# Pair sums on VectorE, regrouped basis products, and a new order at the start and the ends of norms in a four-layer graph network kernel

## The chip, the cores and the metric

The kernel runs on one core of one Trainium2 chip. A core has TensorE (matmuls; PE in the profile, its weight loads PEld), VectorE (DVE), ScalarE (ACT), GpSimd (POOL) and SyncE (SP), and 16 DMA engines that carry what the queues of SP, ACT and POOL issue. The metric is the device time of one execution in microseconds; the median of several runs is compared.

## The reference, cut to what matters

512 nodes with 512 features, 16896 edges, four residual layers, each behind a layer norm and a relu (`h = relu(norm(x))`):

```python
# layer 0: attention over edges, softmax over axis 1 (the HEADS), then a feed-forward net
scores = einsum('nhd,mhd->nhm', q, k) / sqrt(64)          # 8 heads
scores = where(adj[:, None, :] == 0, -1e9, scores)
attn = softmax(scores, axis=1)
h1 = layer_norm(h + einsum('nhm,mhd->nhd', attn, v) @ Wo + bo, g1, be1)
x += layer_norm(h1 + relu(h1 @ W1 + b1) @ W2 + b2, g2, be2)
# layer 1: twice  segment_sum over edges, two linear maps, batch norm, relu, residual
# layer 2: segment_sum with 1/sqrt(degree) on both sides, one linear map
# layer 3: two gated relational layers, for r in 0, 1:
w = einsum('rb,bio->rio', att, basis)                      # 30 bases of 512 x 512
gate = sigmoid(x_j @ gate_w[r]);  msg_r = gate * x_j @ w[r]
out = segment_sum(msg by edge type) + x @ root + bias
```

Because the softmax goes over the 8 heads, its denominator for a pair of nodes is the sum of 8 numbers that lie in 8 different slices of a tile.

## The kernel before, in words

The edges become a 512 x 512 matrix of counts for each edge type. **Start**: the edge indexes (`idx`, `idx2`, the last 4 of 132 chunks) and `x` are loaded, indexes are transposed into `key`, `look_for_strays` sets a flag, and every engine branches on it (L440; the branch is not taken here). The first norm (`norm_relu`) and its four transposes (`flip`) make `hT`. **Counting**: 204 count matmuls (L535) of one-hot rows that VectorE (`hd`, L522, and 3 of 7 `hs`, L528) and ScalarE (4 of 7 `hs`, L526) make. The loop over `order` is a schedule written out by hand: at count numbers in `products` a step of the q, k, v projections is issued, at those in `groups` one step of bases, at those in `begun` the first steps of attention.

**Attention** runs over 8 blocks (2 halves of the queries by 4 tiles of keys). Pass j of its loop issues `weigh(j)` (L630 reciprocal, L631 product, VectorE), `scores(j+2)` (L600, L606 and ScalarE copies), `values(j-1)` (L641), one or two basis steps, `sums(j+1)` (L626: each head's 128 x 256 slice times the identity, added up in one PSUM bank), and `shift(j+2)` (L614 to L621: maximum, subtraction, exponent).

**Bases.** Half of the 30 bases (layer 1 of the gated layers) and 22 (layer 2) are combined on TensorE: a `basis_step` (L244) is 8 matmul instructions; two steps (layer 1) or three (layer 2) close the one PSUM bank `bas`, which ScalarE copies out (L249) before the next step can start, and DMA writes to `summed`. There are 40 steps, strewn over the program. The other bases are added on VectorE: `accumulate` (L268), 1.2 us each, drawn with `advance(more, n)`. Both draw from one ring of four tiles, filled by SP in the order of `USES`.

**Later stages.** Feed-forward; then `gather` (L874: rounded matmuls into four banks `acc`, inside a branch of `exactly`), copies to `aT`, two linear maps, norms with `settle` for layer 1; a gather again for layer 2; then `Layer` twice for layer 3: `look` (gate sums with `gate_rows`, L751 to L754), `begin` (root products, L1014), `messages` (gated halves L1025 and L1026, products L320, copies L1039 and L1041), `end` (L1048).

**What sets the order.** A scheduler orders each engine's instructions by program place and readiness. Those passed through `on` (or `tc.keep_in_program_order`) keep their order among themselves on their engine; the others may be moved. A conditional block is placed as a whole.

Of the kernel before, what the change touches and what calls it, by code (L numbers as in the profile page):

```python
# [17 lines left out]
P = 128  # L18
# [15 lines left out]
USES = "P" * 26 + "VPVVVPPPVPVVPPVVVVPPPPPPPVVVVVVVVVVVV"  # L34
# [40 lines left out]
def gnn_kernel(ctx: ExitStack, tc: tile.TileContext, out: bass.AP, a: dict):  # L75
# [41 lines left out]
    for i, name in enumerate(("dst", "src", "edge_type_2")):  # L117
        nc.sync.dma_start(idx[:, i, :], a[name][0:P * P].rearrange("(c p) -> c p", p=P))
        nc.sync.dma_start(idx2[:, i, :], a[name][P * P:E].rearrange("(c p) -> c p", p=P))
    x = const.tile([P, T, D], F32, name="x")  # L120
    for t in range(T):
        nc.scalar.dma_start(x[:, t, :], a["x"][t * P:(t + 1) * P, :])
# [33 lines left out]
    nc.gpsimd.memset(apart, 1.0)  # L156
# [184 lines left out]

    def stats(v):

        st = stat("st", 6)
        nc.vector.bn_stats(st, v)  # L345
        mv = stat("mv", 2)
        nc.vector.bn_aggr(mv, st)  # L347
        sd = stat("sd")
        nc.scalar.activation(sd, mv[:, 1:2], AF.Sqrt, bias=eps)  # L349
        rstd = stat("rstd")  # L350
        nc.vector.reciprocal(rstd, sd)
        return mv[:, 0:1], rstd
# [16 lines left out]
    far_off = const.tile([P, P], BF16, name="far_off")  # L369
    nc.vector.tensor_scalar(far_off, ident, FAR, None, op0=ALU.mult)  # L370
    deg = const.tile([P, T], F32, name="deg")

    iot = ep.tile([P, N], F16, name="iot")
    nc.vector.tensor_copy(iot, it)
# [4 lines left out]
    for ix, c0 in ((idx, 0), (idx2, P)):  # L379
        n = ix.shape[0]  # L380
        kn = rp.tile([n, 3, P], F32, name=f"kn{c0}")
        nc.vector.tensor_copy(kn, ix)
        for i in range(3):
            nc.tensor.transpose(pk[:, i, c0:c0 + n], kn[:, i, :], ident[:n, :n])
    nc.vector.tensor_copy(key[:, 0:2, :], pk[:, 0:2, :])
    nc.vector.tensor_scalar(key[:, 2, :], pk[:, 2, :], 0.0, LESS, op0=ALU.is_equal, op1=ALU.max)
    nc.vector.tensor_scalar(key[:, 3, :], key[:, 1, :], -1.0, 0.5, op0=ALU.mult, op1=ALU.add)
# [5 lines left out]
    def look_for_strays():  # L393
        over = rp.tile([P, NCH], F32, name="over")
        nc.vector.tensor_tensor(stray, key[:, 0, :], lim[:, 0, :], ALU.is_lt)
        nc.vector.tensor_tensor(over, key[:, 0, :], lim[:, 1, :], ALU.is_ge)
        nc.vector.tensor_add(stray, stray, over)
        some = rp.tile([P, 1], F32, name="some")
        nc.vector.tensor_reduce(some, stray, AX.X, ALU.max)
        p = ps()  # L400
        nc.tensor.matmul(p[0:1, 0:1], lhsT=some, rhs=ones, start=True, stop=True)
        nc.vector.tensor_copy(flag, p[0:1, 0:1])
# [35 lines left out]
    look_for_strays()  # L438
    strays = nc.values_load(flag[0:1, 0:1])
# [5 lines left out]
    made["h"], made["hT"] = big("A"), big("B")  # L445
    for t in range(T):
        norm_relu(made["h"][:, t, :], x[:, t, :])
# [140 lines left out]
    class Block:  # L588
# [33 lines left out]

        def sums(self):
            self.total = bank("ps")[:, :NH]
            for j in range(H):
                on(nc.tensor.matmul(self.total, lhsT=ident, rhs=self.sc[:, j, :], start=(j == 0), stop=(j == H - 1)))  # L626
# [38 lines left out]
    groups = (40, 55, 70, 84, 98, 109, 118, 126, 137, 148, 162, 180, 190)  # L665
    shifts = [None, None]

    def shift_step(i):
        if shifts[i] is None:
# [5 lines left out]
             148: lambda: shift_step(1), 162: lambda: shift_step(1), 184: lambda: blocks[0].sums()}  # L675
# [26 lines left out]
    for j, block in enumerate(blocks):  # L702
        block.weigh()
        if j + 2 < len(blocks):
            blocks[j + 2].scores()
        if j:
            blocks[j - 1].values()
        if j + 1 < len(blocks):
            basis_step(2 if j in (0, 2) else 1)
            blocks[j + 1].sums()  # L710
        if j + 2 < len(blocks):
            for _ in blocks[j + 2].shift():
                pass
# [30 lines left out]
    def gate_rows(l):  # L744

        out = []
        for r in range(2):
            p = ps()
            for k in range(T):
                at = (GW1, GW2)[l] + 2 * k + r  # L750
                nc.tensor.matmul(p[:, ts(k)], lhsT=cols[:, at:at + 1].to_broadcast([P, P]), rhs=ident,  # L751
                                 start=True, stop=True)
            row = rpool.tile([P, 512], F32, tag="row", name="row")
            nc.scalar.copy(row, p)  # L754
            out.append(row)
        return out
# [111 lines left out]
    def gather(ks):  # L868

        def emit(f, c):  # L870
            for k in ks:
                for m in range(T):
                    for i in range(2):
                        nc.tensor.matmul(acc[m], lhsT=f(xn[i][:, k, ts(m)]), rhs=Clx[c][:, k, :],  # L874
                                         start=(k == 0 and i == 0), stop=(k == T - 1 and i == 1))
# [21 lines left out]
    for l in range(2):  # L897
# [50 lines left out]
        if l == 0:  # L948
            settle(l, h2T, 2, xn)
            basis_step(2)  # L950
            settle(l, h2T, 3, xn)
        else:
# [4 lines left out]
            basis_step(1)  # L957

# [23 lines left out]
    first_w = gate_rows(0)  # L982
# [13 lines left out]
    class Layer:  # L996
# [20 lines left out]
        def messages(self, tg, tu, beside):  # L1017
# [11 lines left out]
            for r in range(2):  # L1029
                o = big(tu[r])  # L1030
                for m in range(T):
# [10 lines left out]
                    advance(beside)  # L1042
# [18 lines left out]
    for t in range(1, T):  # L1061
        first.begin(t)
        advance(more, 2)
# [9 lines left out]
    second = Layer(big("A"), big("B"), gate_rows(1))  # L1073
# [11 lines left out]
    for t in (2, 3):  # L1085
        second.begin(t)
        advance(more2, 2)
# [50 lines left out]
```

## Time and profile before

| what | us |
|---|---|
| runs: median (lowest, highest) | 531.04 (528.6, 534.85) |
| the profiled execution, its span | 529.36, 527.6 |
| PE busy | 490.3 (93%) |
| PEld, DVE, ACT, POOL busy | 258.6, 395.3, 195.6, 37.8 |
| start, to the first projection matmul (L459) | 0 to 22 |
| counting | 19 to 111 |
| attention, to the last L626 | 112 to 178 |
| output projection, feed-forward | 178 to 263 |
| layer 1 of the network, layer 2 | 265 to 362, 363 to 397 |
| gated layers | 397 to 524 |

The span is the time between the first and last instruction of the trace; the rest of the profiled time lies around it. The profile's chain of work that ended last goes through TensorE for 69% of the span, VectorE 13%, ScalarE 6%. The DMA engines are busy for 92 to 96% between 40 and 80 us, 62 to 67% in most of attention. The granted TensorE clock is 1.00 in every stretch but 360 to 400 us (0.91) and 400 to 440 us (0.96). A busy PE includes matmuls that wait inside the pipeline, so the distance from one matmul's start to the next is the better measure of its rate.

### The profile page before, as it was taken

Reading aid. Unit: us, or ns where it says so; the run is one execution under the profiler, and the core shown is the slowest. Engines: PE = TensorE matmul, PEld = TensorE weight load, DVE = VectorE, ACT = ScalarE, POOL = GpSimd, SP = SyncE. Lnnn points to the kernel's source line nnn. Section 1 sums busy time; section 2 is a strip of 40 time slices with the busy share of each in tenths; the row PEclk is TensorE's granted clock in tenths of the full one; section 3 lists DMA queues with packets and bytes.
Section 4 is the critical chain, followed back from the end, with each engine's and each line's share of the span. In section 5 each row is a group of like instructions: output and inputs, shape, how many; then the busy total and the mean of one; then the engine's idle time right before and its main releaser. Section 6 shows DMA issues by size and latency. Waiting matters only on the chain.

```text
span 527.6 us, 5796 instructions
## 1 busy us (share of the span) xinstructions
PE 490.3 (93%) x2046; PEld 258.6 (49%) x2046; DVE 395.3 (75%) x738; ACT 195.6 (37%) x318; POOL 37.8 (7%) x81
## 2 busy tenths in 40 slices
PE   1799998799999999999999898999699899999996
PEld 1333343256556546874445344544543385446642
DVE  3855577869897678999786686796579997998611
ACT  3587758753443213224231225124516311123000
POOL 6000000000000011210040000000010100000000
PEclk9999999999999999999999999999799989999999
DMA  7999989798655579768482875766807986420011
GB/s 244 260 219 246 239 237 227 197 249 204 145 128 116 123 161 284 269 174 213 125 255 81 253 235 160 229 174 173 202 2 226 325 203 232 151 89 1 2 40 40
DMA packets 43033, 94.06 MB, mean 178 GB/s; under 512 B 2124, under 2 KB 2520, under 8 KB 43000
## 3 DMA queue, kind: packets, MB, share of 16 engines
q1 hardware_dynamic: 34408, 67.32, 47.9%
q0 software_dynamic: 5712, 21.07, 14.1%
q10 hardware_dynamic: 2880, 5.24, 2.9%
q8 instruction: 20, 0.33, 0.3%
q14 instruction: 13, 0.11, 0.1%
HBM read 88.38 MB, written 5.24 MB: 177 GB/s over the span
## 4 chain that ended last, share of the span: by engine, by line
PE 69%; DVE 13%; issue 7%; ACT 6%; POOL 0%; DMA 0%; ACTq 0%; POOLq 0%; DVEq 0%
PE pr L320 12%; PE acc L1048 10%; PE pg L320 7%; PE ps L626 6%; PE bas L244 5%; PE ps L459 4%; DVE wrel L268 4%; PE acc L874 3%; PE ao L641 3%; PE psc L606 3%; PE acc L1014 3%; PE ao L535 2%; ACT hs L526 2%; DVE st L345 2%; PE acc L320 1%
## 5 line engine op out<-in xcount | busy, mean ns | idle before, releaser
L268 DVE SCALAR_TENSOR_TENSOR wrel<-basis,scal,wrel 128x1024 f32<-128x1024 f32 x60 | 74.1, 1284 | 0.0
L526 ACT ACTIVATE hs<-iot,key 128x512 f16<-128x512 f16 x75 | 48.3, 711 | 7.1 <-PE ao L535 5.4
L522 DVE TENSOR_SCALAR hd<-iot,key 128x32 f16<-128x32 f16 (+1 forms) x132 | 33.3, 295 | 22.2 <-PE ao L535 22.1
L244 PE MATMUL bas<-basis,wide 120*32 120x512 f32 (+1 forms) x320 | 43.7, 600 | 0.9 <-ACT sums L249 0.9
L268 DVE SCALAR_TENSOR_TENSOR w<-basis,scal,w 128x1024 f32<-128x1024 f32 x32 | 39.5, 1279 | 0.9 <-issue 0.9
L535 PE MATMUL ao<-hs,hd 128*32 128x512 f16 x204 | 24.6, 392 | 5.9 <-DVE Bc L544 2.2
L626 PE MATMUL ps<-sc,ident 128*128 128x256 f32 x128 | 29.8, 386 | 0.0
L349 ACT ACTIVATE sd<-mv,eps 128x1 f32<-128x1 f32 x32 | 9.2, 293 | 55.1 <-DVE mv L347 54.1
L626 PEld LDWEIGHTS ps<-sc,ident 128*128 128x128 f32 x128 | 23.7, 190 | 9.5 <-issue 5.8
L621 ACT ACTIVATE sc<-sc 128x2048 f32<-128x2048 f32 (+1 forms) x10 | 15.7, 1567 | 29.5 <-DVE sc L620 29.5
L459 PE MATMUL ps<-bigB,w 128*128 128x512 f32 x56 | 25.9, 605 | 0.0
L320 PE MATMUL pr<-bigE,w 128*128 128x512 f32 x48 | 21.4, 596 | 1.7 <-ACT bigE L913 1.7
L535 PEld LDWEIGHTS <-hd 128*32 128x32 f16 x204 | 7.7, 95 | 26.4 <-issue 15.9
L1094 DVE TENSOR_TENSOR u<-acc,x 128x512 f32<-128x512 f32 x4 | 2.8, 691 | 23.5 <-PE acc L1048 23.5
L320 PE MATMUL pr<-bigD,w 128*128 128x256 f32 x88 | 20.2, 380 | 0.0
L528 DVE TENSOR_SCALAR hs<-iot,key 128x512 f16<-128x512 f16 x57 | 19.6, 353 | 0.4 <-DVEq L440 0.4
L630 DVE RECIPROCAL rec<-ps 128x256 f32<-128x256 f32 x8 | 14.0, 1755 | 7.5 <-PE ps L626 7.5
L620 DVE TENSOR_TENSOR sc<-sc,half 128x2048 f32<-128x2048 f32 (+1 forms) x10 | 18.6, 1863 | 0.2
L608 ACT COPY sc<-psc 128x1024 f32<-128x1024 f32 x16 | 15.9, 1009 | 7.2 <-PE psc L606 5.6
L631 DVE TENSOR_TENSOR sc<-sc,rec 128x2048 f32<-128x2048 f32 x8 | 18.3, 2292 | 0.3
L606 PE MATMUL psc<-bigC,bigD 64*128 64x256 f32 x128 | 18.2, 402 | 0.0
L320 PEld LDWEIGHTS pr<-bigD,w 128*128 128x128 f32 x88 | 16.6, 190 | 3.0 <-ACT bigE L819 0.8
(302 smaller groups left out, 944.9 us busy)
## 6 DMA issues: line engine op xcount, KB each, us to landing
basis<-in_basis SPq DMA_DIRECT2D x32, 960.0 KB
basis<-in_basis SPq DMA_DIRECT2D x23, 1024.0 KB
basis<-in_basis SPq DMA_DIRECT2D x16, 448.0 KB
summed<-sums ACTq DMA_DIRECT2D x16, 256.0 KB
w<-in_W POOLq DMA_DIRECT2D x4, 1024.0 KB, 6.2
row<-in_rows POOLq DMA_DIRECT2D x12, 256.0 KB, 7.6
wrel<-summed POOLq DMA_DIRECT2D x4, 512.0 KB, 8.0
w<-in_conv_W1T POOLq DMA_DIRECT2D x2, 1024.0 KB, 5.8
```

Of the source, the lines that this page charges most:

```text
L244: tc.keep_in_program_order(nc.tensor.matmul(sums[0][32 * j:32 * j + 32, :], lhsT=lhsT, rhs=t[:k, j, :], start=(g == 0), stop=(g == STEPS + ...
L268: on(nc.vector.scalar_tensor_tensor(to[r][:, i:i + 2, :], t[:, i:i + 2, :], scal[:, at:at + 1], to[r][:, i:i + 2, :], op0=ALU.mult, op1=AL ...
L320: nc.tensor.matmul(p, lhsT=lhsT, rhs=rhs, start=(i == 0), stop=(i == len(pairs) - 1))
L459: on(nc.tensor.matmul(p, lhsT=w[:, k, ts(m)], rhs=made["hT"][:, k, :], start=(k == 0), stop=(k == T - 1)))
L522: keep(nc.vector.tensor_scalar(hd[:, :w], iot[:, GW * groups_of[c][0]:GW * groups_of[c][0] + w], key[:, 0, c:c + 1], key[:, 2, c:c + 1], o ...
L526: keep(nc.scalar.activation(hs, iot, AF.Sign, bias=key[:, 3, c:c + 1]))
L528: keep(nc.vector.tensor_scalar(hs, iot, key[:, 1, c:c + 1], None, op0=ALU.is_equal))
L535: keep(nc.tensor.matmul(cnt[b][GW * (g % T):GW * (g % T) + GW, :], lhsT=hd[:, at:at + GW], rhs=hs, start=(c == in_bank[g][b][0]), stop=(c ...
L606: on(nc.tensor.matmul(p[:, b, i, :], lhsT=kT[bs, 2 * q + i, ts(self.mt)], rhs=qT[bs, 2 * q + i, self.ns], start=False, stop=(i == 1)))
L620: on(nc.vector.tensor_sub(s, s, half[:, 0:1, :].to_broadcast([P, H // pieces, NH])))
L626: on(nc.tensor.matmul(self.total, lhsT=ident, rhs=self.sc[:, j, :], start=(j == 0), stop=(j == H - 1)))
L1048: nc.tensor.matmul(self.out[t], lhsT=self.uT[r][:, k, ts(t)], rhs=wrel[r][:, k, :], start=False, stop=(r == 1 and k == T - 1))
```

## The change

1. **Start.** `idx2` loads go to POOL's queue, the edge types to ScalarE's, `x` tiles 2 and 3 to SP's ahead of `Wq`. The key work keeps a written order with the first norm's pieces between it; the branch on strays stands behind the whole first norm. The fill of `apart` moves behind it.
2. **Pairs.** A new `pairs()` adds heads 0 and 4, and 1 and 5, on VectorE (one 128 x 512 addition); `sums` multiplies 6 parts instead of 8.
3. **Groups.** 9 basis steps in counting instead of 13; in attention two at each of j = 0 to 5 and one at j = 6 (13 instead of 9). One step is added at the end of the first norms of layer 1; the last one, at the first gated layer's `look(3)`, then finds nothing left. `USES` follows.
4. **Gather** loops over banks outside and node tiles inside, so that a bank closes before the next begins.
5. **Gate rows** of the second gated layer are made at the end of layer 1's second norms, into `apart`'s memory; all gate-row matmuls keep program order.
6. **Accumulations**: two fewer ahead of `messages` in each gated layer, and two at the first product of each half inside it instead of one.

The diff, with the wrapping of unchanged key and stray operations in `on` cut:

```diff
-USES = "P" * 26 + "VPVVVPPPVPVVPPVVVVPPPPPPPVVVVVVVVVVVV"
+USES = "P" * 26 + "VPVVVPPPVPVVPPPVVVVPPPPPPVVVVVVVVVVVV"
...
-        nc.sync.dma_start(idx[:, i, :], a[name][0:P * P].rearrange("(c p) -> c p", p=P))
-        nc.sync.dma_start(idx2[:, i, :], a[name][P * P:E].rearrange("(c p) -> c p", p=P))
+        (nc.sync, nc.sync, nc.scalar)[i].dma_start(idx[:, i, :], a[name][0:P * P].rearrange("(c p) -> c p", p=P))
+        nc.gpsimd.dma_start(idx2[:, i, :], a[name][P * P:E].rearrange("(c p) -> c p", p=P))
...
-        nc.scalar.dma_start(x[:, t, :], a["x"][t * P:(t + 1) * P, :])
+        (nc.scalar, nc.sync)[t // 2].dma_start(x[:, t, :], a["x"][t * P:(t + 1) * P, :])
...
+    def moments(mv, v, keep=lambda ins: ins):
+        st = stat("st", 6)
+        keep(nc.vector.bn_stats(st, v))
+        keep(nc.vector.bn_aggr(mv, st))
...
+    def first_norm(t):
+        nc.scalar.activation(by4[:, t, 0:1], mv4[:, t, 1:2], AF.Sqrt, bias=eps)
+        on(nc.vector.reciprocal(by4[:, t, 1:2], by4[:, t, 0:1]))
+        on(nc.vector.tensor_scalar(by4[:, t, 2:3], mv4[:, t, 0:1], by4[:, t, 1:2], -1.0, op0=ALU.mult, op1=ALU.mult))
+        nc.scalar.activation(h[:, t, :], x[:, t, :], AF.Relu, bias=by4[:, t, 2:3], scale=by4[:, t, 1:2])
...
+    moments(mv4[:, 0, :], x[:, 0, :], on)
...
+        first_norm(0)
+        moments(mv4[:, 1, :], x[:, 1, :], on)
...
     look_for_strays()
+    for t in range(2, T):
+        moments(mv4[:, t, :], x[:, t, :], on)
+        first_norm(t - 1)
+    first_norm(T - 1)
+    far_off = const.tile([P, P], BF16, name="far_off")
+    on(nc.vector.tensor_scalar(far_off, ident, FAR, None, op0=ALU.mult))
+    nc.gpsimd.memset(apart, 1.0)
     strays = nc.values_load(flag[0:1, 0:1])
...
-    for t in range(T):
-        norm_relu(made["h"][:, t, :], x[:, t, :])
...
+        def pairs(self):
+            v = small.tile([P, N], F32, name="z").rearrange("p (i n) -> p i n", i=2)
+            on(nc.vector.tensor_add(v, self.sc[:, 0:2, :], self.sc[:, 4:6, :]))
+            self.parts = [v[:, i, :] for i in range(2)] + [self.sc[:, j, :] for j in (2, 3, 6, 7)]
...
-            for j in range(H):
-                on(nc.tensor.matmul(self.total, lhsT=ident, rhs=self.sc[:, j, :], start=(j == 0), stop=(j == H - 1)))
+            for j, part in enumerate(self.parts):
+                on(nc.tensor.matmul(self.total, lhsT=ident, rhs=part, start=(j == 0), stop=(j == len(self.parts) - 1)))
...
-    groups = (40, 55, 70, 84, 98, 109, 118, 126, 137, 148, 162, 180, 190)
+    groups = (50, 68, 90, 109, 121, 137, 155, 174, 190)
...
+             148: lambda: shift_step(1), 162: lambda: shift_step(1), 178: lambda: blocks[0].pairs(), 184: lambda: blocks[0].sums()}
...
         block.weigh()
+        if j + 1 < len(blocks):
+            blocks[j + 1].pairs()
         if j + 2 < len(blocks):
             blocks[j + 2].scores()
         if j:
             blocks[j - 1].values()
         if j + 1 < len(blocks):
-            basis_step(2 if j in (0, 2) else 1)
+            basis_step(2 if j < 6 else 1)
             blocks[j + 1].sums()
...
-    def gate_rows(l):
+    def gate_rows(l, out):
...
-                nc.tensor.matmul(p[:, ts(k)], lhsT=cols[:, at:at + 1].to_broadcast([P, P]), rhs=ident,
-                                 start=True, stop=True)
+                on(nc.tensor.matmul(p[:, ts(k)], lhsT=cols[:, at:at + 1].to_broadcast([P, P]), rhs=ident,
+                                    start=True, stop=True))
...
-            for k in ks:
-                for m in range(T):
+            for m in range(T):
+                for k in ks:
...
         if l == 0:
+            basis_step(1)
             settle(l, h2T, 2, xn)
...
             basis_step(1)
+            second_w = gate_rows(1, [apart.bitcast(F32).rearrange("p t n -> p (t n)")[:, N * r:N * r + N] for r in range(2)])
...
-                    advance(beside)
+                    advance(beside, 2 if m == 0 else 1)
...
         first.begin(t)
-        advance(more, 2)
+        if t < 3:
+            advance(more, 2)
...
-    second = Layer(big("A"), big("B"), gate_rows(1))
+    second = Layer(big("A"), big("B"), second_w)
...
         second.begin(t)
-        advance(more2, 2)
+        if t < 3:
+            advance(more2, 2)
```

## The prediction, made before the changed kernel was run

> **What bounds the kernel.** I read the engine totals, the stretches, the chain that ended last, then TensorE, VectorE and ScalarE in order of time. The stretches (columns: span; busy us of PE, PEld, DVE, ACT, POOL; clock; DMA share; GB/s) show TensorE nearly full in counting, attention and the first gated layer, with VectorE second in the last two:
>
> ```profile
> 40.00:60.00 20.00, 19.48 (x98) 7.53 (x100) 11.53 (x45) 14.08 (x25) 0.77 (x1) 1.00 0.96 239
> 120.00:140.00 20.00, 20.00 (x129) 11.76 (x128) 19.52 (x14) 8.21 (x8) 0.00 (x0) 1.00 0.67 166
> 400.00:440.00 40.00, 37.57 (x143) 22.88 (x136) 38.76 (x54) 13.37 (x22) 2.46 (x4) 0.96 0.91 268
> ```
>
> So matmuls removed count, and so do TensorE's few waits. These are the rows that I use (start, duration, what ran, the idle time before it and its releaser), in order of time:
>
> ```profile
> 11.04 0.69 DVE L345 BATCH_NORM_STATS2 st<-x 128x6 f32<-128x512 f32 x1 [3.25 <-DMA x<-in_x]
> 13.45 0.42 DVE L385 COPY key<-psc 128x264 f32<-128x264 f32 x1
> 17.80 1.12 PE L333 MATMUL ps<-ident,bigA 128*128 128x128 f32 x4 [1.52 <-DVEq L440]
> 113.76 1.75 DVE L630 RECIPROCAL rec<-ps 128x256 f32<-128x256 f32 x1
> 115.54 2.29 DVE L631 TENSOR_TENSOR sc<-sc,rec 128x2048 f32<-128x2048 f32 x1
> 115.96 1.07 PE L244 MATMUL bas<-basis,wide 120*32 120x512 f32 x8 [0.70 <-ACT sums L249]
> 116.96 3.72 PE L626 MATMUL ps<-sc,ident 128*128 128x256 f32 x16
> 119.00 0.69 DVE L615 TENSOR_TENSOR half<-half 128x512 f32<-128x512 f32 x1
> 286.35 0.69 DVE L892 TENSOR_TENSOR F<-u,bigC 128x512 fp32r<-128x512 f32 x1 [0.69 <-ACT bigC L891]
> 292.54 7.13 PE L320 MATMUL pr<-bigE,w 128*128 128x512 f32 x16 [1.69 <-ACT bigE L913]
> 366.37 0.59 ACT L754 COPY row<-pr 128x512 f32<-128x512 f32 x1 [1.22 <-PE pr L751]
> 373.06 0.76 PE L874 MATMUL acc<-R,bigC 128*128 128x512 f32 x1 [3.68 <-ACT bigC L972]
> 409.77 9.65 DVE L268 SCALAR_TENSOR_TENSOR wrel<-basis,scal,wrel 128x1024 f32<-128x1024 f32 x8
> 420.14 0.50 PE L320 MATMUL pr<-R,bigB 128*128 128x512 f32 x1 [2.39 <-DVE bigB L1026]
> 422.39 0.63 PE L320 MATMUL pg<-R,bigB 128*128 128x512 f32 x1
> 428.17 0.39 PE L320 MATMUL pr<-R,bigA 128*128 128x512 f32 x1
> 437.19 1.95 PE L751 MATMUL pr<-ident,cols 128*128 128x128 f32 x16
> ```
>
> The reader is to see: the key copy at 13.45 stood behind the statistics of the last x tile, which landed only at 11; the pair sums (L626) are 16 instructions of 0.228 us; and after waits of 3.68 and 2.39 us rounded matmuls come every 0.43 us, not 0.23.
>
> **1. Start: -3.0 us.** Before, every engine passed the branch on strays (L440) at about 17.5. The last x tile now goes on SP ahead of Wq instead of fourth on ScalarE's queue behind it, so it lands by about 5.5 (the third, not behind Wq, was in at 5.2). Three short index loads move to POOL's queue. [...] The ident, lim and iota work queues 2.1 us later on POOL, still ahead of its use. From 6.1 VectorE's fixed order runs: cast 0.55, transposes behind a bn_stats, key copy about 7.5, some nine short operations at 0.2 to 0.35 (2.1), three more statistics at 0.84, four norm tails and far_off (2.0 with the waits for ScalarE): 14.1, branch 14.5. That is 3.0 to 3.3 early; one more flip behind the branch takes some back. Of the queues passed: Wq moves behind two x tiles of 256 KB on SP, but its packets ended at 11.3 and it is wanted at about 19; the edge types' 64 KB go ahead of x on ScalarE's queue, 0.4 us; the 1.82 us fill of apart on POOL moves behind the norms, where POOL is idle and nothing reads it before 42. Ends -3.8 and -0.5 (software loads 2.5 us later).
>
> **2. Counting: -3.8 us.** Four fewer groups of bases at 0.86 (8 matmuls between counts), and block 0's sums lose 4 of 16 matmuls, 0.91. To 77 us TensorE has about 1 us of waits while ScalarE and VectorE have slack, so those three groups give 2.4 in full; from 78 to 104 counting waits for one-hot rows and the bank change, so the fourth gives 0.5. Ends -4.4 and -1.3. One VectorE addition is hidden (3.1 us idle at 106).
>
> **3. Attention: +3.9 us.** This is where the idea costs. Gains: seven more sums lose 0.91 each, 6.4. Costs: four groups at 0.99, 4.0, and three new waits. (a) pairs() stands in VectorE's order behind weigh(): reciprocal 1.78, product 2.21, addition 0.72 plus a handover, so sums(1) begins at 113.76+4.8 = 118.55, not 116.96: 1.6. (b) At the end sums(7) waits likewise: TensorE has only values and one group to do, 2.9 us from the reciprocal, against 4.8: about 2.0. (c) Two groups in a row with the first closing a bank need ScalarE's copy between, 0.70 in the row at 115.96. With 9 groups behind it, this meets j = 0 to 3; j = 0 lies within (a), three remain: 2.1. Walking the blocks with VectorE at 8.64+0.72 = 9.36 per block and TensorE at 3.2 (scores) + 1.93 (values) + 1.98 (two groups) + 2.74 (sums) = 9.85, plus 0.70 where it applies, the last sums end at 181.9 instead of 178.0, counted from the same last count. The difference from 4.0-6.4+5.7 is the extra VectorE round at the first block. Ends +2.0 and +5.0. Queued behind pairs() are the maxima and the shift of the block after next; they have a full block until their sums. Base loads rise to some 180 GB/s, below counting's 239.
>
> **4. Banks closed in turn (L874): +0.9 us.** The gather over tiles 1 to 3 went tile by tile, just as tile 3 came. Now bank 0 wants tile 3 after four matmuls, at 284.3; VectorE has it at 287.04. TensorE stands 2.5 us in the middle, then 18 matmuls at 0.23 end at 291.4 instead of 288.9; two groups follow (1.9) while banks are copied, so the 1.69 wait at 292.54 goes, and the product starts at 293.3. Ends +0.7 and +2.3 (clock halved).
>
> **5. Group at the first norms' end: 0.** It fills waits of 0.70 and 1.60 at 321 and 326; uncovered it would be 1.0. The group that leaves 407 (1.0) only lengthens the wait for VectorE, so 0.
>
> **6. Gate rows: -1.2 and -1.8 us.** The second layer's 16 matmuls leave 437, where TensorE is full (1.8), for the 3.68 us wait at 373. The first layer's are now ordered after them and leave 364 to 367, where their ScalarE copy at 366.37 pushed the last norm back by 0.77. If both fill the wait, the gather stays at full clock (up to 1.3 less); their copies may stand before ScalarE's norms (0.8 against). Ends for 373: -2.1 and +1.5 (the first rows stay behind the gather, at 383). For 437: -1.8 and -0.9.
>
> **7. Messages: -3.4 us.** Two of the eight accumulations in the row at 409.77 move behind the first message halves: 2x1.2 = 2.4 off the wait of 2.39, down to resuming at 417.7. [...] I take -3.4. Ends -4.1 and -1.0 (the moved ones run ahead of the L1026 rows again). What is late next: the moved accumulations. VectorE has 3.35 us idle at 442 and ends its last one 3.0 before TensorE needs it (497.8 against 500.8), so they fit.
>
> **Sum.** -3.0-3.8+3.9+0.9-1.2-1.8-3.4 = -8.4. The profiled execution has span 527.6 and time 529.36; 519.2 and 521.0 follow. The median of runs is 531.04, 1.7 above the profiled time: **522.6**.
>
> **Rivals.** (A) The sum above, range 517 to 527, chance 0.50. (B) The exchange loses: counting is paced by the one-hot rows, only -1.3, and attention pays +5.0: 522.6+2.5+1.1 = 526.2; for it the waits for rows at 87 to 104, against it ScalarE's 14 us of 20. 0.20. (C) The first layer's gate rows don't find the wait at 373: +1.5 there instead of -1.2, and -0.9 at 437: 526.2; against it, those of 363.85 already ran ahead of their place in the program. 0.09. (D) **Slower**: the new waits in attention bring TensorE's clock down. A third of a block at half clock costs 3.3 us; from three blocks on the gain of 8.4 is gone, at five, 16.5, it is 539.1. For it the drop after 2.39 us; against it the waits of 1.05 and 1.84 in counting, after which the stretch still shows 1.00. 0.16. [...] 0.05.
>
> A difference of about 1% (under 525.7 or over 536.4) is what a measurement of this kernel can tell from none. A is faster by that in 0.44 of its 0.50, B and C, at the border, in 0.08 of 0.29, E in all; D is slower. That makes faster 0.57, within 0.27, slower 0.16. The range runs from 515 (A with its better ends) to 532, over A, B, C and E and the slighter forms of D.
>
> **What would show it.** The branch near 14.5; 12 instead of 16 matmuls in each sums, and waits for VectorE at sums(1) and sums(7); waits of 0.7 for ScalarE between groups at j = 1 to 3; a wait in the gather at 284; L751 near 370 twice; resuming at L1026 with less than 1.7 us idle. I am wrong first if sums wait in every block, if counting doesn't shrink, or if the clock falls below 1.00 before 280.

## The result and the profile after

The changed kernel takes 533.59 us (median of 20 runs, 530.75 to 537.75); the kernel before, run beside it, takes 530.52 us (20 runs, 528.6 to 534.85; the 531.04 that the prediction starts from was the median of the first three). The ratio is 1.0055, with a 95% interval of 1.0031 to 1.0079: slower by 0.55%, 2.9 us. The profiled execution has a span of 529.8 us and a time of 531.57, against 527.6 and 529.36.

The three stretches that were shown of before, now of the changed kernel (span; busy us of PE, PEld, DVE, ACT, POOL; clock; DMA share; GB/s):

```profile
40.00:60.00 20.00, 18.95 (x104) 7.33 (x103) 13.25 (x52) 14.05 (x24) 0.77 (x1) 1.00 0.66 166
120.00:140.00 20.00, 18.59 (x121) 10.16 (x120) 18.33 (x15) 9.90 (x9) 0.00 (x0) 1.00 0.84 189
400.00:440.00 40.00, 39.53 (x147) 21.98 (x146) 39.61 (x67) 15.82 (x26) 2.47 (x4) 1.00 0.72 218
```

In this stretch of counting TensorE is less busy (18.95 against 19.48 us): with work taken away it waits more. In attention it no longer fills the stretch (18.59 against 20.00). Only the message stage is fuller (39.53 against 37.57, clock 1.00 against 0.96).

The rows that answer to those of the prediction, in order of time (start, duration, what ran, the idle time before it and its releaser):

```profile
8.41 0.87 DVE L392 CAST kn<-idx 4x384 f32<-4x384 int32 x1 [3.81 <-DMA idx<-in_edge_type]
...
20.92 1.00 PE L554 MATMUL ao<-hs,hd 128*32 128x512 f16 x5 [1.29 <-ACT hs L545]
...
112.92 1.06 PE L243 MATMUL bas<-basis,wide 120*32 120x512 f32 x8 [0.71 <-ACT sums L248]
...
115.44 1.13 PE L651 MATMUL ps<-z,ident 128*128 128x256 f32 x4 [1.46 <-DVE z L645]
...
175.82 1.53 PE L651 MATMUL ps<-z,ident 128*128 128x256 f32 x4 [1.86 <-DVE z L645]
177.15 3.21 PE L651 MATMUL ps<-sc,ident 128*128 128x256 f32 x8
...
288.71 0.47 PE L898 MATMUL acc<-R,bigC 128*128 128x512 f32 x1 [2.06 <-ACT bigC L915]
...
289.94 0.63 PE L898 MATMUL acc<-R,bigC 128*128 128x512 f32 x1
...
374.31 3.68 PE L777 MATMUL pr<-ident,cols 128*128 128x128 f32 x16
...
378.02 0.58 ACT L779 COPY apart<-pr 128x512 f32<-128x512 f32 x1 [1.06 <-PE pr L777]
378.50 0.67 ACT L351 ACTIVATE sd<-mv,eps 128x1 f32<-128x1 f32 x3
...
380.43 0.47 PE L898 MATMUL acc<-R,bigC 128*128 128x512 f32 x1 [2.44 <-ACT bigC L998]
...
390.25 1.05 PE L777 MATMUL pg<-ident,cols 128*128 128x128 f32 x8
...
415.07 9.65 DVE L267 SCALAR_TENSOR_TENSOR wrel<-basis,scal,wrel 128x1024 f32<-128x1024 f32 x8
...
425.45 0.50 PE L319 MATMUL pr<-R,bigB 128*128 128x512 f32 x1 [0.39 <-DVE bigB L1052]
```

The waits that the prediction named are there: 1.46 at the second sums, 1.86 at the last, 2.06 in the gather, 0.71 between groups. What it did not name is there too. The last sums run at 0.38 us each, the gather's matmuls behind its wait come every 0.43: the granted clock is 0.50 from 176.4 to 179.8 us and 0.51 from 289.1 to 292.5. It is 0.50 again from 374.4 to 377.8, where the gate rows (L777) run. ScalarE's second copy of gate rows (L779 at 378.02) stands ahead of the norms' roots (378.50). The first layer's gate rows stay behind the gather (390.25). The head start of the whole beginning is gone by 20.92, where TensorE waits for one-hot rows from ScalarE.

Milestones in the two traces, in us; a plus is later in the changed kernel:

| milestone | before | after | shift |
|---|---|---|---|
| first Q product starts (L459, now L478) | 21.97 | 21.86 | -0.1 |
| it ends | 27.62 | 25.49 | -2.1 |
| second block's scores start, after the last counts | 110.99 | 107.94 | -3.1 |
| last sums end | 178.09 | 180.36 | +2.3 |
| product after the gather | 292.54 | 297.17 | +4.6 |
| third gather starts | 373.06 | 380.43 | +7.4 |
| first layer-2 product | 383.07 | 392.03 | +9.0 |
| second message product's bank starts | 421.92 | 427.89 | +6.0 |
| last matmul ends | 523.31 | 525.83 | +2.5 |

From this table **theory W** was read: the parts' shifts simply add; the exchange of attention and counting, the gather and the gate rows lose, and the message stage gains. Its rivals are that the losses are the clock's (K), that stages with slack swallow single shifts (S), and that the parts only lose where they meet.

### The profile page after: what moved, and what is told of

It reads as the page before. It is cut to its first block, busy times and chain, and to the rows that moved or that the text cites. A ratio compares the mean times of both kernels' runs of the same rounds, so it can differ in the third digit from the quotient of the medians.

```text
span 529.8 us, 5737 instructions
## 1 busy us (share of the span) xinstructions
PE 484.9 (92%) x2014; PEld 254.3 (48%) x2014; DVE 399.7 (75%) x746; ACT 196.1 (37%) x318; POOL 38.8 (7%) x84
## 4 chain that ended last, share of the span: by engine, by line
PE 70%; DVE 19%; ACT 6%; DMA 3%; issue 2%; POOL 0%; ACTq 0%; DVEq 0%; POOLq 0%
PE pr L319 16%; PE acc L1074 10%; PE pg L319 8%; DVE wrel L267 5%; PE ps L651 5%; PE bas L243 5%; PE ps L478 4%; PE acc L898 3%; PE acc L1040 3%; PE ao L666 3%; PE psc L625 2%; PE ao L554 2%; ACT hs L545 2%; DMA basis<-in_basis 1%; PE ps L490 1%
## 5 line engine op out<-in xcount | busy, mean ns | idle before, releaser
L243 PE MATMUL bas<-basis,wide 120*32 120x512 f32 (+1 forms) x320 | 42.2, 601 | 2.9 <-ACT sums L248 2.1
L554 PE MATMUL ao<-hs,hd 128*32 128x512 f16 x204 | 22.6, 386 | 8.3 <-ACT hs L545 5.7
L351 ACT ACTIVATE sd<-mv,eps 128x1 f32<-128x1 f32 x28 | 8.0, 294 | 54.1 <-DVE mv L344 53.1
L478 PE MATMUL ps<-bigB,w 128*128 128x512 f32 x56 | 25.9, 606 | 0.7 <-ACT bigD L480 0.7
L898 PE MATMUL acc<-R,bigC 128*128 128x512 f32 x32 | 14.6, 455 | 4.5 <-ACT bigC L998 2.4
L319 PE MATMUL pr<-w,bigE 128*128 128x512 f32 x40 | 17.8, 593 | 0.0
```

The costliest lines, as they stand in the source:

```text
L243: tc.keep_in_program_order(nc.tensor.matmul(sums[0][32 * j:32 * j + 32, :], lhsT=lhsT, rhs=t[:k, j, :], start=(g == 0), stop=(g == STEPS + ...
L319: nc.tensor.matmul(p, lhsT=lhsT, rhs=rhs, start=(i == 0), stop=(i == len(pairs) - 1))
L478: on(nc.tensor.matmul(p, lhsT=w[:, k, ts(m)], rhs=made["hT"][:, k, :], start=(k == 0), stop=(k == T - 1)))
L554: keep(nc.tensor.matmul(cnt[b][GW * (g % T):GW * (g % T) + GW, :], lhsT=hd[:, at:at + GW], rhs=hs, start=(c == in_bank[g][b][0]), stop=(c ...
```

## The experiments

Every ratio below is to the kernel before, run beside it on the same chip, with its 95% interval; a change in us is the ratio's on 530.6. Of each edit only the core is repeated; the rest stands in the diff above.

### One part of the change at a time

**The start** (queues, keys first, fixed order of the norms' statistics).

```
-        nc.sync.dma_start(idx2[:, i, :], ...)
+        nc.gpsimd.dma_start(idx2[:, i, :], ...)
...
+    for t in range(2, T):
+        moments(mv4[:, t, :], x[:, t, :], on)
+        first_norm(t - 1)
```

> The kernel before with the new start alone (loads on other queues, keys first, norm statistics in a fixed order); nothing of the computation is left out. Theory W (the parts' shifts read off the two traces simply add): the first Q product ends 2.1 us earlier, as in the changed kernel, and nothing later gives it back, so -2.1 us. The prediction's own working: -3.0. Rival S (the later stages have slack in front of a transfer and swallow a head start): the milestones at 111 and 178 are not moved, 0. In the trace the branch stands near 15.5 and the short index loads land near 8.4.

Measured: 530.40 us, 0.9985 [0.9965, 1.0006]. Faster by 0.8 us at best guess, and no difference is not excluded. The branch came where expected, and the first Q product starts at 22.18 against 21.97 before. So nothing was left of it at TensorE, and the -2.1 of the changed kernel's trace was its clock: the eight matmuls at the product's start took 3.70 us there, 5.16 here and 5.72 before. The clock records of the traces begin with full clock at 19.4 us in the changed kernel's, 25.2 here and 26.1 before, so that -2.1 is not the new start's, which this run has too.

**The exchange** (pair sums on VectorE, four groups of bases from counting to attention), whole and in its two halves.

```
+            on(nc.vector.tensor_add(v, self.sc[:, 0:2, :], self.sc[:, 4:6, :]))
...
-    groups = (40, 55, 70, 84, 98, 109, 118, 126, 137, 148, 162, 180, 190)
+    groups = (50, 68, 90, 109, 121, 137, 155, 174, 190)
...
-            basis_step(2 if j in (0, 2) else 1)
+            basis_step(2 if j < 6 else 1)
```

> The kernel before with the pair sums on VectorE and four groups of bases moved from counting to attention, alone. Theory W: counting gains only 1.0 us by the last count, attention pays 5.3 until the last sums, +4.3 at the first product after attention and at the end. The prediction's working: -3.8 +3.9, +0.1. Rival K (the loss is the clock's, in the last sums only, and is a chance of where the wait falls): the last sums run at 0.23 us each, and the total is +2.5.

Measured: 536.62 us, 1.0110 [1.0070, 1.0149], +5.8 us. In its trace the first Q product ends 1.3 us earlier than before, the last counts another 0.9, and the last sums end 3.1 later: attention costs 5.3. The trace's end is 6.1 later; most of the rest comes in the gated layers, where VectorE waits 3.39 us for a load (see "The message stages").

> The kernel before with four groups of bases moved from counting to attention, all eight parts still summed on TensorE: one half of the exchange. Theory P (counting is paced by the one-hot rows that ScalarE and VectorE make, so TensorE's removed matmuls become waits there, while each group costs its full time in attention): 0 at the start of the first sums at 105, +4.0 for the groups and up to +2.1 for the waits for ScalarE's copy in attention, +6 at the last sums. The prediction's working (counting gains 2.9 from the groups): +3.2 or less. The end shows the same as the last sums, give or take the message stage, whose length differs from run to run.

Measured: 536.83 us, 1.0127 [1.0094, 1.0160], +6.7 us. From the first sums' start to the last sums' end it takes 79.0 us against 72.8 before, +6.2; four groups of 0.99 and three waits of 0.70 make 6.1. In counting nothing was won. The table of TensorE's waits between 40 and 105 us (who waited for whom: us in total, times, the longest) says why, first of the kernel before, then of this one:

```profile
PE ao L535 <- DVE Bc L544: 2.2, 2, 1.8
PE ao L535 <- DVE hd L522: 1.3, 2, 1.0
PE ao L535 <- ACT hs L526: 0.5, 2, 0.2
```

```profile
PE ao L535 <- ACT hs L526: 3.8, 5, 1.9
PE ao L535 <- DVE Bc L544: 2.2, 2, 1.8
```

The waits for ScalarE's one-hot rows rose from 0.5 to 3.8 us. The Q, K and V products show when: the one that starts at 77.14 before starts at 75.18 here, 2.0 earlier (0.8 of it from the first Q's clock), and the first sums then start only 0.8 earlier, at 104.49. By then three groups, 2.6 us of work, had gone, and TensorE was 1.2 us ahead. It gave that back in two places, rows of groups_only:

```profile
86.35 0.39 PE L535 MATMUL ao<-hs,hd 128*32 128x512 f16 x2 [1.90 <-ACT hs L526]
...
104.18 0.38 PE L535 MATMUL ao<-hs,hd 128*32 128x512 f16 x1 [1.20 <-ACT hs L526]
```

Why ScalarE could not deliver earlier shows in a stretch of the kernel before (span; busy us of PE, PEld, DVE, ACT, POOL; clock; DMA share; GB/s), in which it is busy for 9.30 of 9.30 us. Between the one-hot rows it makes exponentials of the first block (L621) and copies scores of the second (L608):

```profile
79.90:89.20 9.30, 8.03 (x63) 2.86 (x61) 6.11 (x19) 9.30 (x15) 0.00 (x0) 1.00 0.92 229
```

> The other half of the exchange: pair sums on VectorE as in the changed kernel (behind the weighing), the groups of bases left where they were. Theory P: -0.9 in the first sums, then VectorE's round, 9.1 to 9.4 us, paces the blocks instead of TensorE's 9.88, -3.5 over seven, less the waits at the second and the last sums, +1.5 to +3.4: -1 to -3 at the last sums. Rival K (waits for VectorE drop TensorE's clock in several blocks): sums at 0.38 us and a time above that of before, +2.

Measured: 530.55 us, 0.9988 [0.9968, 1.0008]: no difference that can be told. Rows of its timeline, the waits at the first, second and last sums:

```profile
106.49 1.13 PE L632 MATMUL ps<-z,ident 128*128 128x256 f32 x4 [1.14 <-DVE z L626]
...
118.83 1.13 PE L632 MATMUL ps<-z,ident 128*128 128x256 f32 x4 [1.46 <-DVE z L626]
...
174.29 1.35 PE L632 MATMUL ps<-z,ident 128*128 128x256 f32 x4 [3.15 <-DVE z L626]
175.43 3.40 PE L632 MATMUL ps<-sc,ident 128*128 128x256 f32 x8
```

The sums lose 8 x 0.91 = 7.3 us of matmuls. The three waits return 5.75 of it, and the last sums at half rate (4.5 instead of 2.8 us) another 1.7, so that nothing is left. Between those waits a block takes VectorE 9.24 us (its reciprocals start at 151.07 and 160.31), and TensorE keeps step.

> As pairs_only, but each pair sum stands in VectorE's order ahead of the weighing of the block before it, where it is ready early. Theory P: the waits of the sums for the pair sum go (1.5 at the second, some 1.9 at the last), so this is 1 to 3 us under pairs_only, and -4 at the last sums against before. If VectorE's round sets the pace anyway, rival V, the order changes nothing: within 0.5 us of pairs_only.

```
-        block.weigh()
         if j + 1 < len(blocks):
             blocks[j + 1].pairs()
+        block.weigh()
```

Measured: 542.50 us, 1.0204 [1.0152, 1.0255], +10.8 us. Both theories missed. Its timeline:

```profile
125.70 0.69 DVE L626 TENSOR_TENSOR z<-sc 128x512 f32<-128x512 f32 x1 [1.98 <-ACT sc L621]
...
128.12 1.13 PE L632 MATMUL ps<-z,ident 128*128 128x256 f32 x4 [1.09 <-DVE rec L636]
...
150.79 2.08 PE L632 MATMUL ps<-z,ident 128*128 128x256 f32 x4 [2.49 <-DVE rec L636]
```

The pair sum needs the exponentials, which ScalarE makes last in a block's round. Put ahead of the weighing, it draws them into VectorE's own chain: VectorE waits some 2.0 us for ScalarE in every block, the round grows to 11.3 us, and TensorE waits for the pair sums ("DVE rec" is the last releaser seen, the pair sum is just ahead of it). Behind the weighing, as in the change, the exponentials were done by then.

**The gather, closed bank by bank.**

```
-            for k in ks:
-                for m in range(T):
+            for m in range(T):
+                for k in ks:
```

> The kernel before with the gather's loops exchanged (banks closed in turn), alone. Theory W: a wait of about 2.1 us after the first four matmuls of bank 0, then matmuls at 0.43 us for some 3 us: +2.4 at the product after the gather and at the end. The prediction's working: wait 2.5, full rate after it, +0.9. Rival S: conv stage swallows it, 0.

Measured: 533.18 us, 1.0044 [1.0024, 1.0065], +2.3 us. Theory W holds, the slack of rival S doesn't exist. The wait, and a matmul of those behind it that come at half rate (granted clock 0.50 from 286.8 to 290.2):

```profile
285.69 0.47 PE L874 MATMUL acc<-R,bigC 128*128 128x512 f32 x1 [2.06 <-ACT bigC L891]
...
286.95 0.63 PE L874 MATMUL acc<-R,F 128*128 128x512 f32 x1
```

Seven matmuls from 286.95 on come every 0.43 us, the rest every 0.23.

**The gate rows.**

```
+            second_w = gate_rows(1, [apart.bitcast(F32)...])
...
-    second = Layer(big("A"), big("B"), gate_rows(1))
+    second = Layer(big("A"), big("B"), second_w)
```

> The kernel before with the gate rows moved and held in program order, alone. Theory W: both copies of the second layer's rows stand ahead of the norms' square roots on ScalarE, and the first layer's matmuls stay behind the gather: at the product after the gather +2.4 -0.8 +1.8 = +3.4, at the end -1.8 of it back: +1.6. The prediction's working: -3.0. Rival K: the loss at 373 is only the cold matmuls of the rows (3.7 us instead of 1.95), +1.7 at the gather and -0.1 at the end.

Measured: 529.90 us, 0.9986 [0.9962, 1.0009], -0.7 us, between the theories. Zero is not excluded. The second layer's rows found the wait and ran at full rate, and the copies (369.53 and 370.42) did not hold up the third gather: it starts at 372.40, 0.7 earlier than before. But the first layer's rows stayed behind it:

```profile
372.40 0.47 PE L871 MATMUL acc<-R,bigC 128*128 128x512 f32 x1 [2.02 <-ACT bigC L970]
...
383.67 1.05 PE L750 MATMUL pg<-ident,cols 128*128 128x128 f32 x8
384.56 1.06 PE L750 MATMUL pr<-ident,cols 128*128 128x128 f32 x8
```

These 1.8 us are what the move saves at 437. In the changed kernel it was worse, 3.68 us for the same 16 matmuls after a wait of 2.00, and the copies then did stand ahead of the norms.

**The message stages.**

```
-                    advance(beside)
+                    advance(beside, 2 if m == 0 else 1)
...
-        advance(more, 2)
+        if t < 3:
+            advance(more, 2)
```

> The kernel before with the accumulations of the message stages moved behind the first halves, alone. Theory W: the wait of 2.39 us for VectorE before the second product falls to about 0.4 and the full clock stays; -3.4 at the end, and up to 2 more, since VectorE's first accumulation of the second layer, which stood waiting for the load of its sums for 0.95 to 5.0 us in the profiles so far, comes later and finds its load. Rival: the moved accumulations are late at the stage's end: -1.0.

Measured: 526.59 us, 0.9910 [0.9876, 0.9944], -4.8 us. Besides the 2.39 us wait and the half clock, a second thing went. It is seen best where it was worst, in the trace of start_only, whose message stage is that of the kernel before:

```profile
421.12 0.80 PE L319 MATMUL pr<-R,bigB 128*128 128x512 f32 x1 [2.39 <-DVE bigB L1045]
...
431.25 1.28 DVE L267 SCALAR_TENSOR_TENSOR w<-basis,scal,w 128x1024 f32<-128x1024 f32 x1 [5.01 <-DMA w<-summed]
...
433.28 0.47 PE L319 MATMUL pg<-R,G 128*128 128x512 f32 x1 [1.88 <-DVE bigC L1058]
```

VectorE's first accumulation of layer 2 stands in its order ahead of a copy that TensorE waits for, and itself waits for the load of its sums: 5.01 us here. This run, at 535.88 us, is the slowest of the 22 of start_only (528.72 to 535.88). In the eight profiles with the old message stage VectorE is idle for 0.95 to 5.01 us ahead of this accumulation (where it was 0.95, in before, the profile names no load). With the message edits the accumulation comes later, in messages_only behind four of the first layer's that follow the halves instead of one, and in eight of ten profiles it finds its load; in msg_pairs_mid and msg_gates_late VectorE still idles 1.29 and 1.54 us there. The runs of messages_only lie between 524.2 and 527.0. That this load is what scatters the runs is not shown: the changed kernel has the message edits and no such wait, and its runs lie 7 us apart.

### The parts mended, on top of the message edits

The four kernels of this section ran beside each other on one chip. A difference against messages_only, which ran on another, is one of two ratios whose intervals overlap (for msg_pairs_mid barely). But all six runs of each of the first three lie below all six of the last one, msg_group (526.34 to 526.90), so that each of the three gains.

> The message edits (526.6 us alone) and, of the exchange, pair sums for the blocks 2 to 6 only: blocks 0, 1 and 7 sum all eight parts on TensorE, and no group of bases is moved. Theory P: with pairs in all blocks VectorE's round of 9.24 us paced the blocks, and 1.1, 1.5 and 3.2 us were lost at the first, second and last sums, the last ones at half clock; without these three waits the last sums end 3 us sooner than before, so 523.6. Rival V (VectorE is late by the same amount elsewhere): within 1 us of 526.6.

```
-        if j + 1 < len(blocks):
+        if 1 <= j < 6:
             blocks[j + 1].pairs()
```

Measured: 522.77 us, 0.9843 [0.9809, 0.9878]: 3.6 us under the message edits alone by the two ratios. From the first sums' start to the last sums' end it takes 69.2 us against 72.8 before, the same 3.6. The last sums wait 0.63 instead of 3.15 us and run at full clock. So VectorE could carry the pair sums; what cost were the two ends of the chain and the groups.

> The message edits (526.6 alone) and the gate rows moved, but with the second layer's two copies on VectorE behind the gather instead of on ScalarE ahead of the norms, and the first layer's rows free to run early. Theory W: all 16 matmuls lie in the wait ahead of the third gather, one copy (0.6 us) still stands ahead of the norms, +1.0 there and -1.8 at the end of the first messages: -0.8 to -1.8, 525.3. Rival: the copies weren't what cost; as gates_only, within 0.7 of 526.6.

```
-            nc.scalar.copy(out[r], p)
+            hold.append((out[r], p))
...
+    for to, p in held:
+        nc.vector.tensor_copy(to, p)
```

Measured: 524.53 us, 0.9879 [0.9846, 0.9912], -1.6 us against the message edits. All 32 row matmuls lie ahead of the gather.

> The message edits (526.6 alone) and the new start, with the three short index loads on the hardware queues beside their long ones instead of GpSimd's. Theory Q (the software queue held the keys back: they landed 5.9 us after issue): the short loads are in by 4.5, everything up to the branch comes 3 us earlier, branch near 12.5, and the first Q product starts 2 us earlier: 524.6. Rival N (three flips, their copies and the last norm, now behind the branch and ahead of the one-hot rows on ScalarE, set the first product, with the load of Wq): branch earlier, but Q within 1 us, 525.6 to 526.6.

```
-        nc.gpsimd.dma_start(idx2[:, i, :], ...)
+        (nc.sync, nc.sync, nc.scalar)[i].dma_start(idx2[:, i, :], ...)
```

Measured: 524.25 us, 0.9868 [0.9834, 0.9903], -2.2 us. Theory Q holds:

```profile
4.73 0.51 DVE L392 CAST kn<-idx 4x384 f32<-4x384 int32 x1 [0.16 <-DMA idx<-in_src]
...
19.75 5.56 PE L478 MATMUL psc<-bigB,w 128*128 128x512 f32 x8
```

The short loads are cast at 4.73 instead of 8.41, and the first Q product starts 2.2 us earlier than before. No two kernels differ in these queues alone, so this rests on the traces: with the short loads on GpSimd's queue the product starts at 21.86 to 22.18 in five profiles, with them on SP's and ScalarE's at 19.75 here and 20.79 in best (where VectorE's cast of the long loads took 2.70 instead of 0.40 us). With the old start, the same code in eleven profiles, it is 20.03 to 23.26, since the statistics of the last `x` tile start between 9.12 and 12.33 there: the 11.04 that the prediction read was one draw of many.

> The message edits (526.6 alone) and the group of bases at the first norms' end. The prediction's working: 0. Theory W: the load order around it shifts, and VectorE waits for a whole base after the second gather; +0.6 to +1.2.

Measured: 526.74 us, 0.9915 [0.9883, 0.9948]: +0.3 us against the message edits, so alone the moved group costs nothing that can be told.

### Do the losses add?

> The changed kernel with two of its parts taken back: the four groups of bases stay in counting, and the gather's loops are as before. If the parts add as they did alone (groups +6.7 at the end alone, gather +2.4): 533.6 less 8 to 9, 524.5 to 525.5, 1.1% under the kernel before. Rival (the parts don't add; the loss of the changed kernel comes of their meeting): over 528.

Measured: 531.66 us, 1.0009 [0.9985, 1.0034]. Theory W failed here: taking back parts that cost 9.0 us alone won about 2. Its trace is level with before until the product after the second gather (+0.3 at 334) and 6.0 us late at the third. Rows of after_less, then the same accumulation in the changed kernel:

```profile
331.75 4.87 DVE L267 SCALAR_TENSOR_TENSOR wrel<-basis,scal,wrel 128x1024 f32<-128x1024 f32 x4 [2.24 <-DMA basis<-in_basis]
...
337.27 7.97 PE L319 MATMUL pr<-bigE,w 128*128 128x512 f32 x14 [2.16 <-DVE bigE L935]
```

```profile
334.78 4.87 DVE L267 SCALAR_TENSOR_TENSOR wrel<-basis,scal,wrel 128x1024 f32<-128x1024 f32 x4 [0.38 <-DMA basis<-in_basis]
```

The group at the first norms' end puts its base ahead of the whole base that VectorE adds up here. VectorE waits 2.24 us for it, its copies of the gather's banks stand behind the accumulations, and TensorE waits 2.16 us and then runs at half rate (granted clock 0.50 from 338.5 to 341.9). In the changed kernel, some 5 us later at this place, the base was nearly there: 0.38. Two more kernels test whether that is the cause.

> The changed kernel less three parts: the four groups of bases, the gather's loops and the group at the first norms' end. Theory D (in after_less the moved group put its base ahead of a whole base that VectorE adds up at 331.75; this came 2.2 us late, held VectorE's copies of the gather's banks, and TensorE waited 2.2 us and ran at half clock after it; 5 us lost there): this runs 5 to 7 us under after_less, 524.5 to 526.5, as the parts measured alone add up to. Rival (the meeting of start, pairs and gates costs it): over 529.

```
         if l == 0:
-            basis_step(1)
             settle(l, h2T, 2, xn)
```

Measured: 524.21 us, 0.9853 [0.9815, 0.9890], 8.3 us under after_less by the two ratios. The line is the cause, and theory D holds, though its price was set at 5 to 7.

> The changed kernel with only the group at the first norms' end taken back. Theory D: there the 5 us lost before in attention and the gather let the late base land in time (VectorE waited 0.38 us for it), so this part cost little: 533.6 less 0 to 1.5. Rival: it costs as much as in after_less, 528.5.

Measured: 532.12 us, 1.0021 [0.9997, 1.0046]: 1.8 us under the changed kernel by the ratios, whose intervals overlap. One and the same line costs nothing that can be told alone, about 1.8 in the changed kernel at best guess, and 8 in after_less. That the changed kernel comes late enough to find its base is read from the waits, 0.38 against 2.24. Why its base came 1.1 us later in after_less than in msg_group (1.10 us waited there) stays open.

### The version that beats both

> The edits that gained, together: message stages (-4 alone), pair sums for blocks 2 to 6 (-3.8 on top of it), gate rows with late copies (-2.1), the start with the short index loads on hardware queues (-2.3); groups, gather and base loads' order as before. If they add: 518.4. Rival (a later stage waits for a load that now comes too late): 521 or more.

Measured: 517.97 us, 0.9767 [0.9721, 0.9812]: 2.3% faster than before, 2.9% than the changed kernel. The mended gains add, as far as ratios with intervals of about 2 us to each side can tell: -4.8, -3.6, -1.6 and -2.2 make -12.2, and -12.4 was measured.

## Why the prediction was wrong

Predicted 522.6, measured 533.6, 1.6 us above its range. The changes it forecast and what each part gave alone, in us:

| step | forecast | measured alone | its interval |
|---|---|---|---|
| 1 start | -3.0 | -0.8 | -1.9 to +0.3 |
| 2 and 3 counting and attention | +0.1 | +5.8 | +3.7 to +7.9 |
| 4 gather | +0.9 | +2.3 | +1.3 to +3.4 |
| 5 group at the norms' end | 0 | +0.3, in the changed kernel about +1.8 | about 2 to each side |
| 6 gate rows | -3.0 | -0.7 | -2.0 to +0.5 |
| 7 messages | -3.4 | -4.8 | -6.6 to -3.0 |
| sum | -8.4 | +2.1, with 1.8 for step 5 +3.6; as a whole +2.9 | whole: +1.6 to +4.2 |

That the sum comes near the whole does not show that the parts add: after_less says that they don't.

**The step that failed** is the second: "To 77 us TensorE has about 1 us of waits while ScalarE and VectorE have slack, so those three groups give 2.4 in full". ScalarE's busy share of 14 in 20 us between 40 and 60 was read as slack. But TensorE takes the one-hot rows in order, and the groups between the counts were what covered the making of them. TensorE gained 1.2 us by 77 and gave it back where ScalarE is busy without a break (79.9 to 89.2), in waits for `hs` that rose from 0.5 to 3.8 us. The four groups gave nothing; counting gave only the first sums' 0.9, not 3.8. This is rival B's first half; its price for it, 2.5, was still 0.4 too small.

**Attention** was right in its mechanism. The groups' 6.1 us (4.0 and 2.1) measured 6.2, the waits (a) 1.6 and (b) 2.0 measured 1.46 and 1.86. What was missing is the half rate that came behind one of these waits: +5.3 by the trace instead of +3.9. In the changed kernel it met the last sums (granted clock 0.50, 4.5 instead of 2.8 us), in exchange_only the second ones (2.05 us for four matmuls instead of 1.13). Rival D named this mechanism, from three blocks on; here it met one round.

**Start.** The 6.1 us that its order of work starts from is an estimate: the third short load issued at about 2.1, and in 4.0 us later, as the 32 KB of `cols` were in before. No run shows it for the short loads. In the changed kernel they were in 3.4, 4.5 and 5.8 us after issue (`cols` 6.7); the last, issued at 2.51, was cast at 8.41. With them on SP's and ScalarE's queues, in msg_start_sp, it was cast at 4.73, and the gain appeared, 2.2 us at best guess. The other error was "one more flip behind the branch": three of the four were, and their copies and the last norms run on ScalarE ahead of the one-hot rows.

**Gather.** The wait was forecast at 2.5 and measured 2.06; the half rate behind it, left to the upper end of +2.3, came. By the prediction's own times, 293.3 against 292.54, its working gives 0.8, not 0.9. **Gate rows.** Rival C's mechanism came: the first layer's rows stayed behind the gather (1.8). Its price was too high, since the gather started 0.7 earlier and not 1.5 later. **Messages** were right: the forecast lies within the measured interval. Its -3.4 is 2.4 for the wait and 1.0 for the rate, and no run shows that 1.0: before, eight matmuls behind the wait came every 0.43 us, 1.6 us lost (an estimate against 0.23), and in messages_only, behind waits of 0.36 and 0.37 us, the same eight come every 0.23. At best guess the forecast was too small by 1.4, and the late load of the second layer's sums, which was not seen, is argued to be the rest; its sign, an idle time of 0.95 at 426, was in the profile.

**Range and signs.** Start, counting, attention and gather came out near, at or past the worse ends that the prediction gave them. All its worse ends together make +5.1, or 536.1; its range stopped at 532, as if they would not come together. Of its three signs of being wrong two came: counting shrank by no more than 0.9, and the clock fell before 280 (at 176.4).

**The clock.** The half rate that was read behind the wait of 2.39 us came again behind waits of 2.06 (gather), 1.86 (last sums) and 2.16 us (after_less), with a granted clock of 0.50 in each. Its price should have been set at each new wait of this length. Behind waits of 1.46 and 1.84 us it came in some traces and not in others; the last section has the counts.

## What to carry to other kernels

Removing work from the busiest engine pays only as far as its suppliers are ahead: ask of each wait that remains who delivers next, and how its time of delivery compares with the work that is taken away. A supplier's share of busy time over a long stretch does not tell; look at it just ahead of the wait, and at what else stands in its order. A chain across engines (exponentials, pair sum, weighing) cost most here at its first and last round, where nothing covered it (waits of 1.46 and 3.15 us in pairs_only), so leave the ends in the old form. Losses can cover one another; take a change apart in both directions, alone and out of the whole, before a part is called free.

## What was not expected of the hardware

**One wait, two outcomes.** A wait of 1.46 us ahead of the second sums was followed by full rate in the changed kernel (four matmuls in 1.13 us) and by half rate in exchange_only (2.05 us). In the clock records of the eighteen traces the granted clock changes only at whole multiples of 3.41 us from its first record: in the changed kernel's it is 1.00 for 157.01 us (46 times 3.41), 0.50 for 3.41, 1.00 for 109.23 (32 times) and 0.50 for 3.41 again. In counting, TensorE waits 1.84 us for the change of banks (L544) in all eighteen, and in seven a stretch at half clock follows. Cut at those multiples, the wait is split over two stretches in before and lies in one in gates_only, and only there the next stretch has a granted clock of 0.50 (span; busy us of PE, PEld, DVE, ACT, POOL; clock; DMA share; GB/s):

```profile
90.90:94.30 3.40, 2.74 (x7) 1.04 (x6) 2.29 (x7) 2.41 (x4) 0.00 (x0) 1.00 0.97 207
94.30:97.70 3.40, 2.01 (x25) 0.93 (x24) 2.93 (x7) 2.72 (x6) 0.00 (x0) 1.00 0.69 184
97.70:101.10 3.40, 3.40 (x14) 1.44 (x8) 3.40 (x13) 1.52 (x2) 0.00 (x0) 1.00 0.67 168
```

```profile
93.00:96.40 3.40, 1.36 (x16) 0.69 (x19) 2.09 (x4) 3.40 (x8) 0.00 (x0) 1.00 0.95 257
96.40:99.80 3.40, 3.40 (x18) 1.37 (x9) 3.40 (x11) 0.85 (x2) 0.00 (x0) 0.50 0.43 133
```

Over all traces there are 2560 such stretches at full clock. By the rows' starts and ends (an estimate, as TensorE's ends are modelled) TensorE idles for less than 1.5 us in 2486 of them, and none is followed by half clock; for 2.0 us or more in 29, and all are; in the 45 between, 15 are. In exchange_only the 1.46 and a wait of 0.70 us fell into one stretch, 2.16 us; in the changed kernel that stretch has 1.7. These are counts of this kernel's traces; why they come out so is not shown. A full stretch at half clock loses about 1.7 us of matmuls (an estimate, half of 3.41; the last sums of the changed kernel took 4.5 instead of 2.8).

**The start of the clock.** The eight matmuls at the start of the first Q product took 3.70, 5.13, 5.16, 5.56 and 5.72 us in five profiles, though they are the same work. The clock records begin at 19.4 us where they took 3.70, at 25.2 where 5.16 and at 26.1 where 5.72. Why they begin where they do is not shown.

**Small loads.** Twelve rows of 128 indices on GpSimd's queue in the changed kernel, 6 KB in three loads, landed 3.4, 4.5 and 5.8 us after the issue of each; the last was issued at 2.51 us and cast at 8.41.
